# Attention with a conditioning token on one core: six loads of Wk issued by ScalarE, the token's product with Wk placed behind that with Wq, and another split of the first swap round

## The chip, the core and the metric

The kernel runs on one core of one Trainium2 chip. The core has TensorE (PE, with weight loads shown as PEld), VectorE (DVE), ScalarE (ACT), GpSimd (POOL) and SyncE (SP), which only issues transfers. ScalarE and GpSimd can issue transfers too, from their own instruction streams. The metric is the time of one execution in microseconds on the device, as the median of several runs.

## What is computed

The input x has 8 batch elements of 512 rows and 512 columns. There are 16 heads of 32 columns. A conditioning token of 512 numbers per batch element is projected with the same Wq and Wk and added to every row of Q and K:

```python
Q = _split_heads(x @ Wq.T + bq)
K = _split_heads(x @ Wk.T + bk)
V = _split_heads(x @ Wv.T + bv)
tQ = _split_heads(tokens @ Wq.T + bq)
tK = _split_heads(tokens @ Wk.T + bk)
cQ = Q + tQ
cK = K + tK
scores = jnp.einsum('bhqd,bhkd->bhqk', cQ, cK) / jnp.sqrt(jnp.float32(HEAD_DIM))
attn = jax.nn.softmax(scores, axis=-1)
out = jnp.einsum('bhqk,bhkd->bhqd', attn, V)
```

The result, with heads put back beside each other, is added to x. All data are float32.

## The kernel before

**Tasks.** A task t is one batch element and one group of four heads (128 columns), so there are 32 tasks, and t // 4 is the batch element. Each task needs the scores twice: once with queries along the partitions, to get the row maxima (`row_max`, L641 on TensorE, L589 and L650 on VectorE) and the sums of the exponentials (`denominators`, L693 on ScalarE), and once with keys along the partitions, for the product with V (`exponentials`, `weighted`, L808).

**Kept tasks.** For the tasks 2 to 28 (`KEPT`, 27 of them) half of the exponentials are not computed a second time. ScalarE writes them to SBUF in the first pass, VectorE turns them in 32 by 32 blocks (`turn_kept`, L660), and transfers swap the blocks across partitions in place. There are six pairs of places to swap (`APART`), and `swap_kept` does this in three rounds of six copies of 128 KB: round 0 puts one place of a pair aside, round 1 fills it from the other, round 2 fills the other from the copy put aside. Each copy waits for its own pair's copy in the round before. Rounds 0 and 1 of task t + 1 are issued at the end of step t, round 2 in the second third of step t + 1. TensorE reads the kept half in `weighted` of that task, one step later, in the second half of its L808 products. All copies of round 2 are issued by GpSimd; those of round 1 by SyncE; of round 0 SyncE issues the first three pairs and GpSimd the last three (L674).

**The projections.** They use a product scheme with seven block products in place of eight (`first_by_others`, `other_products`, L461). Sums of x blocks for it are made once for each batch element by `combine_x` (L387 to L391) on GpSimd, in the step whose number is 0 modulo 4. GpSimd also scales and adds to the output (L881, L882), adds the bias (L204), splits the maxima (L707 to L710) and makes the sums of a product's parts (L535 to L537, L1220, L1221, L1209). The order of the instructions on each compute engine is the order of the program text. SyncE's transfers are issued in the order that a scheduler gives them.

**The start.** Wq is loaded in four transfers of 128 rows and turned on TensorE (`transpose_w`, L313), with copies to SBUF by ScalarE (L322) and VectorE (L320). The first 128 rows of Wk come through ScalarE's queue and are turned on TensorE too. The other 384 rows come in sixteen loads of 48 KB, in pieces of 128 bytes, so that VectorE alone can turn them (`turn_w`, L963): four quarters cc of the input columns with four row blocks h each (L270). Wv follows in sixteen loads of 64 KB. The token's products are `condition("q")` and `condition("k")` (L902), four small products of which quarter cc needs the turned quarter cc of the weight. Their results are copied by ScalarE (L904), turned back on TensorE (`condition_end`, L889), summed over the quarters and joined with the bias (L911, L917), and then added to Q and K as these leave PSUM (L417, L419). Between them stands the projection of Q for task 1, one quarter at a time (`project_qk_part`, L404). The first row maxima (L641) need K of task 0.

Of the kernel before, what the change touches and what calls it, by code (L numbers as in the profile page):

```python
# [17 lines left out]
def kernel(  # L18
# [38 lines left out]
    nc = tc.nc  # L57
# [5 lines left out]
    HG = P // HD  # L63
    NP = HG // 2
    NS = S // P
    NC = D // P
# [96 lines left out]
    def spread(a, d):  # L163

        return a.rearrange("(f j) d -> j f d", j=BL)[:, :, d : d + BL]

    def load_block(n):

        b, cc = divmod(n, NC)
        if b < B:  # L170
            xs[n] = xp.tile([P, NB, BL], F32, tag="x", name=f"x_{n}")
            for h in range(HG):
                nc.sync.dma_start(xs[n][h * BL : (h + 1) * BL], spread(x[b], cc * P + h * BL))
# [89 lines left out]
    nc.scalar.activation(table, ones[:, :1], AF.Exp)  # L263
    load_w("q", Wq, nc.sync, [2, 3])

    for n, w, f in (("k", Wk, HG), ("v", Wv, 0)):
        wn = ws[n].rearrange("p c (f e) -> p c f e", e=BL)
        for cc in range(NC):
            for h in range(HG):
                nc.sync.dma_start(  # L270
                    wn[h * BL : (h + 1) * BL, cc, f:], spread(w, cc * P + h * BL)[:, f:]
                )
    bvl = const.tile([P, 1], F32, tag="bvl", name="bvl")
    nc.sync.dma_start(bvl, bv.rearrange("(g p o) -> g p o", g=G, o=1)[G - 1])
    bvs = const.tile([P, G, BL], F32, tag="bvs", name="bvs")
# [74 lines left out]
    def transpose_x(n, pt, leaves=nc.vector.tensor_copy):  # L350

        b, sc = divmod(n, NS)
        if b >= B:
            return
        if sc == 0:
            xT[b] = xtp.tile([P, NC, S], F32, tag="xT", name=f"xT_{b}")
        for cc in range(NC):
            nc.tensor.transpose(
                pt[:, cc * P : (cc + 1) * P], xs[n][:, cc * P : (cc + 1) * P], ident
            )  # L360
        leaves(xT[b][:, :, sc * P : (sc + 1) * P], pt.rearrange("p (c s) -> p c s", c=NC))
        if n > 1:
            load_block(n + 2)
# [38 lines left out]
    def project_qk_part(t, n, cc, pt, at=slice(0, S)):  # L402
        b, g = divmod(t, G)
        nc.tensor.matmul(  # L404
            pt[:, at],
            wT[n][:, cc, g * P : (g + 1) * P],
            xT[b][:, cc, at],
            start=(cc == 0),
            stop=(cc == NC - 1),
        )  # L410

    def project_qk_end(t, n, pt):
        b, g = divmod(t, G)
        o = pair_of(t, n)[:, t % 2, :]
        add = tok[:, "qk".index(n), g, b : b + 1]
        if n == "q":
            nc.vector.tensor_scalar(o, pt, add, None, ALU.add)  # L417
        else:
            nc.scalar.activation(o, pt, AF.Identity, bias=add)  # L419
        qkT[n, t] = o  # L420
# [243 lines left out]

    def swap_kept(t, move, last=nc.gpsimd):

        def part(a, g):
            return kept[t][a * BL : (a + 1) * BL, g].rearrange("p c h s -> p (c h s)")

        for n, (a, g) in enumerate(APART):  # L670
            at = (n + 2) % HG * BL
            aside = between[at : at + BL, n // HG].rearrange("p i s -> p (i s)")
            to, of = [(aside, part(a, g)), (part(a, g), part(g, a)), (part(g, a), aside)][move]
            (last if move == 2 or move == 0 and n >= 3 else nc.sync).dma_start(to, of)  # L674

    def denominators(t, qc, w=HG, js=range(HG)):

# [220 lines left out]
    def condition(n, pt):  # L898


        for cc in range(NC):
            nc.tensor.matmul(pt[cc * HD : (cc + 1) * HD, :], condT[:, cc, :], wT[n][:, cc, :])  # L902
        part[n] = early[:, 1 + "qk".index(n), :]
        nc.scalar.copy(part[n], pt)  # L904

    def condition_end(n, pt, on):

        i = "qk".index(n)
        untranspose(part[n], pt)
        sum4 = const.tile([P, NC, B], F32, tag=f"sum4{n}", name=f"sum4_{n}")  # L910
        nc.vector.tensor_reduce(  # L911
            sum4,
            pt.rearrange("p (d c e) -> p d e c", d=NC, c=NC)[:, :, 0:B, :],
            AX.X,
            ALU.add,
        )
        on.tensor_tensor(  # L917
            tok[:, i], sum4, bias2[:, i, :].unsqueeze(2).broadcast_to([P, NC, B]), ALU.add
        )
# [5 lines left out]
    bank = bank_of  # L925
# [4 lines left out]
    def first_part(n, pt, h):  # L930
        for cc in range(NC):
            project_qk_part(0, n, cc, pt, slice(h * HS, (h + 1) * HS))
# [16 lines left out]
    first_part("q", pq, 0)  # L949
    transpose_x(2, bank(0))  # L950
    transpose_x(3, bank(3), nc.scalar.copy)
    first_part("k", pk, 0)
    for half in range(2):
        combine_x(0, half, nc.gpsimd)
# [6 lines left out]
    def turn_w(n, ccs, rows=slice(0, D)):  # L961
        for cc in ccs:
            nc.vector.transpose(wT[n][:, cc, rows], ws[n][:, cc, rows])  # L963

    turn_w("k", range(NC), slice(P, D))
    condition("q", bank(6))
    project_qk_part(1, "q", 0, bank(7))
    condition_end("q", bank(1), nc.vector)
    project_qk_end(0, "q", pq)
    condition("k", bank(5))  # L970
    project_qk_part(1, "q", 1, bank(7))
    condition_end("k", bank(0), nc.gpsimd)
    project_qk_end(0, "k", pk)
# [157 lines left out]
    def thirds(t, made):  # L1131
# [16 lines left out]
        for i in (1, 2):  # L1148
# [6 lines left out]
            if i == 1:  # L1155
                if t + 1 in KEPT:
                    swap_kept(t, 2)
                split_max(t + 1)
                if t + 1 in KEPT:
                    turn_max(t + 1)  # L1160
                else:
                    swap_kept(t, 2)
# [17 lines left out]
            if i == 2:  # L1180
                if r == 0:
                    combine_x(b + 1, 1, nc.gpsimd)
                load_residual(t + 1)
                if t + 1 in KEPT:
                    for move in range(2):
                        swap_kept(t + 1, move)
            else:
                bias_residual(t)
                if r == 0:
                    combine_x(b + 1, 0, nc.gpsimd)  # L1190
# [46 lines left out]
    for t in range(1, T - 3):  # L1237
# [6 lines left out]
        for i, item in enumerate(items):  # L1244
# [3 lines left out]
            w = 0 if alone else HG  # L1248
# [46 lines left out]
    def latest_pair(of, among):  # L1295
        pairs = [(j, j + 1) for j in of if j + 1 in of and among & {j, j + 1}]
        return max(pairs, key=lambda p: order.index(p[0]) + order.index(p[1]))

    last = latest_pair(order, {order[7]})
# [59 lines left out]
    t = T - 3  # L1359
# [20 lines left out]
    t = T - 2  # L1380
# [27 lines left out]
    t = T - 1  # L1408
# [103 lines left out]
```

## Time and profile before

| | us |
|---|---|
| median of 3 runs | 666.72 |
| lowest and highest | 666.71, 668.23 |
| the profiled execution, whole | 667.76 |
| its span in the trace | 666.0 |
| busy: TensorE, VectorE | 652.7 (98%), 589.9 (89%) |
| busy: ScalarE, GpSimd | 542.0 (81%), 423.6 (64%) |

The profile is one execution. Its page gives the busy time of each engine, the chain of work that ended last (followed back from the last instruction, at each step to what released it), the costliest groups of instructions by source line, and the transfers by issuing line. The trace behind it can be asked for timelines, for the chain in a stretch, for waits and for transfers. In a timeline row stand the start in microseconds, the length, the engine, the source line, the operation, what it writes and reads, and in brackets how long the engine was idle before it and what ended that. Matmuls are pipelined and their ends are modelled, so starts are the safer figure on TensorE.

The granted TensorE clock in this execution is 0.996 of full speed over the span.

### The profile page before, as it was taken

How to read it: one execution, taken by the hardware profiler on the slowest of the kernel's cores; microseconds unless marked ns; L12 is line 12 of the kernel's file. 1: busy time of each engine (PE TensorE's matmuls, PEld its weight loads, DVE VectorE, ACT ScalarE, POOL GpSimd, SP SyncE). 2: the span in 40 equal slices, each digit the busy share in tenths (PEclk: the TensorE clock that was granted, in tenths of full speed). 3: DMA queues.
4: the chain of work that ended last, by engine and by line, in shares of the span. 5: the costliest groups of instructions: out<-in, count | busy, mean ns of one | idle time of the engine just before them, and what ended most of it. 6: DMA issues, size and time to landing. Idle time of an engine off the chain costs nothing.

```text
span 666.0 us, 24768 instructions
## 1 busy us (share of the span) xinstructions
PE 652.7 (98%) x9812; PEld 349.4 (52%) x9812; DVE 589.9 (89%) x821; ACT 542.0 (81%) x1378; POOL 423.6 (64%) x668
## 2 busy tenths in 40 slices
PE   9999999999999999999999999999999999999993
PEld 7345445555555555555555555555555555555421
DVE  3698899999999999998999999999999989995793
ACT  2479988889888888988888898888889888887771
POOL 3541345787666876659757696667875597576531
PEclk9999999999999999999999999999999999999998
DMA  6633157778777787877897787779877757786111
GB/s 178 105 51 63 31 122 161 163 165 187 173 152 174 161 190 154 189 156 167 171 190 167 169 191 172 160 150 170 196 165 176 169 133 175 149 181 138 18 18 32
DMA packets 246183, 97.14 MB, mean 146 GB/s; under 512 B 228842, under 2 KB 229354, under 8 KB 246068
## 3 DMA queue, kind: packets, MB, share of 16 engines
q1 hardware_dynamic: 232644, 62.65, 49.3%
q0 software_dynamic: 11664, 31.87, 17.3%
q8 instruction: 77, 1.26, 0.9%
q10 hardware_dynamic: 1760, 1.05, 0.5%
q14 instruction: 38, 0.31, 0.1%
HBM read 19.75 MB, written 8.39 MB: 42 GB/s over the span
## 4 chain that ended last, share of the span: by engine, by line
PE 95%; DMA 2%; SPq 1%; DVE 1%; issue 0%; DVEq 0%
PE psum L461 43%; PE psum L641 19%; PE psum L808 15%; PE psum L777 7%; PE psum L792 3%; PE psum L766 3%; PE psum L748 2%; SPq L270 1%; PE psum L404 1%; DMA w_q<-in_L_cond_Wq_dram 1%; PE psum L745 1%; PE psum L1336 1%; PE psum L818 1%; DMA store<-in_x_dram 1%; DMA w_k<-in_L_cond_Wk_dram 0%; PE psum L843 0%
## 5 line engine op out<-in xcount | busy, mean ns | idle before, releaser
L693 ACT ACTIVATE psum<-psum,nmax 128x512 f32<-128x512 f32 x263 | 174.8, 670 | 5.0 <-DVE nmax L589 3.9
L589 DVE TENSOR_REDUCE nmax<-psum 128x1 f32<-128x512 f32 x219 | 140.5, 678 | 22.2 <-PE psum L641 19.6
L693 ACT ACTIVATE store<-psum,nmax 128x512 f32<-128x512 f32 x190 | 130.3, 700 | 33.3 <-DVE nmax L589 23.8
L650 DVE TENSOR_REDUCE nmax<-psum 128x2 f32<-128x1024 f32 x127 | 153.7, 1211 | 1.3 <-PE psum L641 1.3
L674 POOL DMA_DIRECT2D store<-store x243 | 121.7, 504 | 48.1 <-DMA store<-store 36.2
L641 PE MATMUL psum<-kT,qT 32*128 32x512 f32 x1024 | 146.7, 616 | 0.0
L787 ACT ACTIVATE store<-psum 128x512 f32<-128x512 f32 x216 | 111.5, 603 | 22.6 <-PE psum L777 22.6
L660 DVE STREAM_TRANSPOSE store<-store 128x1024 f32<-128x1024 f32 x108 | 129.5, 1217 | 0.0
L808 PE MATMUL psum<-store,v 128*32 128x256 f32 x1728 | 99.3, 381 | 0.0
L808 PEld LDWEIGHTS psum<-store,v 128*32 128x32 f32 x1728 | 53.2, 110 | 54.1 <-ACT wT_q L628 19.7
L641 PEld LDWEIGHTS psum<-kT,qT 32*128 32x128 f32 x1024 | 57.8, 183 | 37.3 <-issue 20.2
L881 POOL TENSOR_TENSOR res<-res,recs 128x512 f32<-128x512 f32 x30 | 31.4, 1047 | 69.0 <-DVE res L880 68.9
L693 ACT ACTIVATION_READ_ACCUMULATOR psum<-psum,nmax 128x1 f32 x263 | 56.3, 214 | 0.0
L777 PE MATMUL psum<-qT,kT 32*128 32x256 f32 x864 | 55.8, 373 | 0.0
L461 PE MATMUL psum<-wc_v,xc 128*32 128x256 f32 x768 | 47.7, 379 | 0.0
L204 POOL TENSOR_TENSOR xr<-xr,bvs 128x512 f32<-128x512 f32 x30 | 38.4, 1279 | 12.2 <-DMA x<-in_x_dram 11.4
L461 PE MATMUL psum<-xc,wc_k 128*32 128x256 f32 x720 | 44.5, 379 | 0.0
L461 PE MATMUL psum<-xc,wc_q 128*32 128x256 f32 x720 | 44.5, 379 | 0.0
L777 PEld LDWEIGHTS psum<-qT,kT 32*128 32x128 f32 x864 | 42.3, 184 | 3.4
L693 ACT ACTIVATION_READ_ACCUMULATOR store<-psum,nmax 128x1 f32 x190 | 40.8, 215 | 0.0
L882 POOL TENSOR_TENSOR res<-res,xr 128x512 f32<-128x512 f32 x30 | 38.4, 1279 | 2.4
L758 ACT ACTIVATE store<-psum 128x512 f32<-128x512 f32 x56 | 28.9, 603 | 9.3 <-PE psum L748 7.2
(198 smaller groups left out, 1046.3 us busy)
## 6 DMA issues: line engine op xcount, KB each, us to landing
store<-store SPq DMA_DIRECT2D x243, 128.0 KB, 2.8
store<-store POOLq DMA_DIRECT2D x243, 128.0 KB, 3.7
out_dram<-res SPq DMA_DIRECT2D x122, 64.0 KB, 3.6
xr<-in_x_dram SPq DMA_DIRECT2D x120, 64.0 KB, 3.4
x<-in_x_dram SPq DMA_DIRECT2D x112, 64.0 KB, 3.0
w_q<-in_L_cond_Wq_dram SPq DMA_DIRECT2D x4, 256.0 KB, 5.3
w_v<-in_L_cond_Wv_dram SPq DMA_DIRECT2D x16, 64.0 KB, 2.5
w_k<-in_L_cond_Wk_dram SPq DMA_DIRECT2D x16, 48.0 KB, 3.0
```

The source lines that it names most:

```text
L204: nc.gpsimd.tensor_tensor(xr[t], xr[t], bias, ALU.add)
L461: nc.tensor.matmul(pt[r], still[:, r], moving, start=(kc == kcs[0]), stop=(kc == kcs[-1]))
L589: nc.vector.tensor_reduce(nmax[t][:, qc, j : j + 1, 0], pt, AX.X, ALU.max, negate=True)
L641: nc.tensor.matmul(pt, qkT["q", t][r, qc * P : (qc + 1) * P], qkT["k", t][r, :], start=True, stop=True,)
L650: nc.vector.tensor_reduce(nmax[t][:, qc, pr * 2 : pr * 2 + 2, 0], pt, AX.X, ALU.max, negate=True)
L660: nc.vector.transpose(e, e)
L674: (last if move == 2 or move == 0 and n >= 3 else nc.sync).dma_start(to, of)
L693: nc.scalar.activation(to, of, AF.Exp, bias=nmax[t][:, qc, j, :], accum_out=sums[t][:, qc, j, :],)
L777: nc.tensor.matmul(bank[j][:, i * HS : (i + 1) * HS], qkT["k", t][r, kc * P : (kc + 1) * P], qkT["q", t][r, rest], start=False, stop=(i == 1),
L787: nc.scalar.activation(e[:, i, :], bank[pr * 2 + i], AF.Exp)
L808: nc.tensor.matmul(pt[j * HD : (j + 1) * HD, half * HS : (half + 1) * HS], vs[b % 2][:, kc, (g * HG + j) * HD : (g * HG + j + 1) * HD], e, ...
L882: nc.gpsimd.tensor_tensor(y, y, xr.pop(t), ALU.add)
```

## The change

Three things change. First, the loads of Wk and Wv are written as a function, `load_spread`, with a choice of quarters, row blocks and queue. SyncE issues the first ten loads of Wk (quarters 0 and 1 and half of quarter 2) and then Wv. ScalarE issues the other six, and its instruction stream has them behind the copy of the fourth x tile and ahead of its scaled copy of Wq's third part. Second, `condition("k")` moves ahead of the first quarter of the projection and of `condition_end("q")`, so that TensorE has L902 for Wk directly behind L902 for Wq. Third, in round 0 of `swap_kept` GpSimd issues none of the six copies for tasks whose number is 1 modulo 4, and the last five for all others; SyncE has the rest.

```diff
-    for n, w, f in (("k", Wk, HG), ("v", Wv, 0)):
+    def load_spread(n, w, f, ccs, queue=nc.sync, hs=range(HG)):
         wn = ws[n].rearrange("p c (f e) -> p c f e", e=BL)
-        for cc in range(NC):
-            for h in range(HG):
-                nc.sync.dma_start(
+        for cc in ccs:
+            for h in hs:
+                queue.dma_start(
                     wn[h * BL : (h + 1) * BL, cc, f:], spread(w, cc * P + h * BL)[:, f:]
                 )
+
+    load_spread("k", Wk, HG, (0, 1))
+    load_spread("k", Wk, HG, (2,), nc.sync, (0, 1))
+    load_spread("v", Wv, 0, range(NC))
...
     def swap_kept(t, move, last=nc.gpsimd):
 
+        later = 6 if t % 4 == 1 else 1
...
-            (last if move == 2 or move == 0 and n >= 3 else nc.sync).dma_start(to, of)
+            (last if move == 2 or move == 0 and n >= later else nc.sync).dma_start(to, of)
...
     transpose_x(3, bank(3), nc.scalar.copy)
+    load_spread("k", Wk, HG, (2,), nc.scalar, (2, 3))
+    load_spread("k", Wk, HG, (3,), nc.scalar)
     first_part("k", pk, 0)
...
     condition("q", bank(6))
+    condition("k", bank(5))
     project_qk_part(1, "q", 0, bank(7))
     condition_end("q", bank(1), nc.vector)
     project_qk_end(0, "q", pq)
-    condition("k", bank(5))
     project_qk_part(1, "q", 1, bank(7))
```

## The prediction

> **What bounds the kernel now.** I read the chain of waits for the whole span first, then the same chain for single stretches, then the timelines of the engines that it names.
>
> ```profile
> PE 95%; DMA 2%; SPq 1%; DVE 1%; issue 0%; DVEq 0%
> ```
>
> TensorE's own work is 95% of the chain that ends last. An edit elsewhere is therefore worth only what TensorE now waits for. It waits in two kinds of place that the change touches. The first is the start, here in the chain for 0 to 26 us (start, length, what):
>
> ```profile
> 9.87 1.11 SPq L270
> ...
> 11.54 2.07 SPq L270
> ...
> 17.24 2.33 DMA w_k<-in_L_cond_Wk_dram
> ...
> 19.70 0.59 DVE wT_k L963
> ...
> 20.33 1.05 PE psum L902 x2
> 21.38 1.06 PE psum L404 x2
> 22.44 0.44 PE psum L889 x4
> 22.87 1.72 PE psum L404 x4
> 24.59 1.07 PE psum L641 x8
> ```
>
> From 9.87 to 19.57 the end of the chain is SyncE handing out the sixteen loads of Wk one by one, and the flight of the sixteenth. Its turn on VectorE (L963) releases the last quarter of the token's product with Wk (L902) at 20.33. TensorE's timeline of the same stretch shows what ran before:
>
> ```profile
> 16.28 1.06 PE L902 MATMUL psum<-wT_q,condT 128*32 128x512 f32 x8
> 17.28 1.12 PE L404 MATMUL psum<-xT,wT_q 128*128 128x512 f32 x2
> 18.24 0.60 PE L889 MATMUL psum<-ident,store 128*128 128x128 f32 x4
> 18.77 1.06 PE L902 MATMUL psum<-wT_k,condT 128*32 128x512 f32 x6
> ```
>
> Start to start, the product with Wq takes 1.00 us, a quarter of a projection 0.96, the turning back of the token's Q 0.53. From 16.28 to 22.87 there are 6.59 us.
>
> The second place recurs. In one row-maxima burst (L641) per batch element the chain is longer from the fourth time on; the first row is the same burst one batch element earlier, without the excess:
>
> ```profile
> 239.62 0.92 PE psum L641 x8
> ...
> 316.71 1.34 PE psum L641 x7
> ...
> 394.22 1.38 PE psum L641 x6
> ...
> 471.77 1.58 PE psum L641 x8
> ...
> 549.53 1.50 PE psum L641 x8
> ```
>
> The excess over 0.92 is 0.42, 0.46, 0.66 and 0.58, together 2.12 us. The timelines of GpSimd, ScalarE, VectorE and the weight loads around the last one show its cause:
>
> ```profile
> 541.04 1.29 POOL L391 TENSOR_TENSOR xc<-xT,xc 128x512 f32<-128x512 f32 x1
> 541.12 0.66 DVE L880 STREAM_TRANSPOSE res<-psum 128x512 f32<-128x512 f32 x1
> 542.27 1.52 POOL L674 DMA_DIRECT2D store<-store  x3
> 543.32 0.62 ACT L533 COPY qT<-psum 128x512 f32<-128x512 f32 x1
> 543.81 1.06 POOL L881 TENSOR_TENSOR res<-res,recs 128x512 f32<-128x512 f32 x1
> 546.18 0.74 POOL L535 TENSOR_TENSOR qT<-qT 128x256 f32<-128x256 f32 x1
> 547.68 0.73 POOL L537 TENSOR_TENSOR qT<-qT 128x256 f32<-128x256 f32 x1
> 548.45 1.41 DVE L486 SCALAR_TENSOR_TENSOR qT<-psum,tok,qT 128x512 f32<-128x512 f32 x2 [0.26 <-POOL qT L537]
> 549.91 0.29 PEld L641 LDWEIGHTS psum<-kT,qT 32*128 32x128 f32 x2 [0.35 <-DVE qT L486]
> ```
>
> GpSimd works without a pause through the combination of x (L391), three issues of swap copies (L674, 0.51 us each), the scaled output (L881) and the sums of Q (L535 to L537). VectorE waits for the last sum, and TensorE for VectorE to leave the PSUM bank.
>
> **The change, part one: six loads of Wk on ScalarE.** In both kernels' instruction lists a transfer from SyncE or ScalarE waits until the one issued eight places earlier by the two together has landed. The profile shows such a wait at the sixth load of Wk:
>
> ```profile
> SPq L270 <- DMA w_q<-in_L_cond_Wq_dram: 1.0, 1, 1.0
> ```
>
> The new loads stand behind ScalarE's copy of x (L361) and ahead of its scaled copy of Wq (L322):
>
> ```profile
> 9.89 0.58 ACT L361 COPY xT<-psum 128x512 f32<-128x512 f32 x1 [2.99 <-PE psum L358]
> 14.22 0.60 ACT L322 ACTIVATE wT_q<-psum 128x512 f32<-128x512 f32 x1 [3.75 <-PE psum L313]
> ```
>
> They can begin at 10.47 and hide in an idle stretch of 3.75 us. How soon they land is not in the trace; I bound it by the Wk loads issued before and after 13.6 us, in the transfer views of 9.8 to 13.6 and 13.65 to 17.7 us (last column: median from issue to landing):
>
> ```profile
> w_k<-in_L_cond_Wk_dram SPq DMA_DIRECT2D x3, 48.0 KB, 3.6
> ...
> w_k<-in_L_cond_Wk_dram SPq DMA_DIRECT2D x8, 48.0 KB, 2.3
> ```
>
> The first goes out near 10.7 and the second near 11.5, each behind an earlier landing. The fifth waits for the first, the sixth for the second. With 3.6 us of flight the sixth is issued at 15.1 and, with 2.3 of its own, Wk is complete at 17.4. With 2.3 throughout the sixth goes at 13.8; SyncE's tenth load, which waits for its sixth (issued at 9.87, 3.6 in flight: 13.5; up to 14.2 if SyncE's 2.07 us at 11.54 stays), then ends it, at 16.5 at the latest. The other bound is today's 19.57.
>
> What that is worth: a landing L lets TensorE begin the last quarter of L902 at L + 0.76 (19.57 to 20.33 now). Since the product with Wk now stands ahead of the projection quarter and the turning back of Q, 1.05 + 0.96 + 0.53 + 1.06 + 0.44 = 4.04 us follow until the point that is now at 22.87. So the gain is 22.87 - 4.04 - 0.76 - L = 18.07 - L. It cannot exceed TensorE's own work from 16.28: 1.00 + 1.00 + 0.96 + 0.53 + 1.06 + 0.44 = 4.99, so 6.59 - 4.99 = 1.60. L = 17.4 gives 0.7, L = 16.5 gives 1.57, L = 19.57 gives a loss of 1.5: the reordering takes away the 1.49 us of work that now covers the wait. I take 0.8, close to 17.4, since the flights before 13.6 were the long ones.
>
> ScalarE's wait delays L322: issued at 15.1, the sixth load ends near 15.6, so L322 ends at 16.2. TensorE wants it at 16.28. This costs nothing, with only 0.1 us of cover; each later microsecond on ScalarE is one on TensorE. Behind it come only the copies of the token's products. SyncE's loads of Wv and x move up by six issues of about 0.5 us; I find nothing that waits for them now, and if they slow Wk, the bound of 19.57 contains it.
>
> A rule speaks against this part. The Trainium skill, Perfetto Trace Analysis, section "DMA Instruction — HWDGE (DVE, Sync)", says that an issue locks the descriptor generator, which two sequencers share. By it ScalarE's issues would queue behind SyncE's; that is the second rival below. At the start of this trace the two overlap at full speed, which disagrees, though these are loads of 2 KB rows:
>
> ```profile
> 0.73 0.41 ACTq L158 DMA_DIRECT2D store<-in_x_dram  x1
> 0.74 0.41 SPq L231 DMA_DIRECT2D w_q<-in_L_cond_Wq_dram  x1
> ```
>
> **Part two: the first swap round.** For each kept task whose number is 1 modulo 4 (6 of 27), GpSimd loses its three issues of the first round, 1.52 us. That is the stretch shown. L881 can then follow L391 at 542.33, since L880 is done at 541.78; L535 would come at 544.66, after L533 (543.94). Everything to L537 is 1.52 us earlier, more than the excess of at most 0.66, so the four excesses go: 2.1 us. The lower bound is VectorE's own wait, 0.26 in each of four places: 1.0 us. No upper bound above 2.12 is seen. SyncE issues those three copies itself, 1.6 us, and no longer waits for GpSimd's.
>
> In the other 21 tasks GpSimd issues two more, 1.0 us. They hide in the pause in front of L881, as here:
>
> ```profile
> 561.62 1.04 POOL L881 TENSOR_TENSOR res<-res,recs 128x512 f32<-128x512 f32 x1 [2.83 <-DVE res L880]
> ```
>
> Without that cover the cost would be 21 times 1.0. Late next would be the copies themselves; that is the last rival.
>
> **The sum.** The profiled execution took 667.76 us for a span of 666.0, so 1.76 lie around it. Less 0.8 and 2.1 it is 664.9. It is 1.04 above the median of 666.72, so a median run should come at **663.8 us**; the other cases are set against the median too. Its own range, with 0.0 to 1.6 and 1.7 to 2.1, is 663.0 to 665.0.
>
> **Rivals.** (1) Taking GpSimd's lateness away shortens VectorE's wait only, because the bank is then held by the rest of VectorE's queue. For it: the trace names 0.26 us there. Against: the same burst at 239.62 has no excess although VectorE does the same work. Gain 1.0 + 0.8: 664.9, within 0.3%.
>
> (2) The two queues generate descriptors in turn. SyncE's 2.07 us at 11.54 would hold ScalarE's second load until 13.6; alternating at 0.51 us, the sixth would end at 18.2 and land at 20.0. L322 would end at 18.8, and the product with Wk would start its last quarter at 20.76, so the prologue loses 20.76 + 4.04 - 22.87 = 1.9 us. With the 2.1 gained later: 666.5, no change. Against it stand the overlapping issues above.
>
> (3) Slower: the kept exponentials arrive late. A task's third swap round waits for its second and that for its first, and TensorE reads the result half-way through L808. GpSimd's copies land later than SyncE's:
>
> ```profile
> store<-store SPq DMA_DIRECT2D x243, 128.0 KB, 2.8
> store<-store POOLq DMA_DIRECT2D x243, 128.0 KB, 3.7
> ...
> 548.35 2.96 POOL L674 DMA_DIRECT2D store<-store  x6
> ...
> 556.20 3.59 PE psum L808 x64
> ```
>
> Here the third round is issued by 551.31 and lands by 555.0, and is read at 556.20 + 1.8 = 558.0: 3.0 us to spare. Two issues more (1.0) and 0.9 of landing make 1.9, so it does not bite. From 3.0 on each microsecond costs 21: at 3.3 the time is 663.8 + 6.3 = 670.1. For it: the flights differ from burst to burst.
>
> (4) The change does not do what it says at the start: the bound of eight transfers in flight makes ScalarE's loads as late as SyncE's (18.07), so it gains nothing. Then 666.72 - 2.1 = 664.6, just faster.
>
> **How the numbers follow.** Forecast 0.62, rival (1) 0.13, (2) 0.08, (3) 0.12, (4) 0.05. About 0.3%, 2.0 us, is what a measurement can tell from no change, so faster means below 664.7. Of the forecast's cases nine in ten are faster; with most of (4) that makes 0.60. The rest of it, (1) and (2) make 0.28 within 0.3%. Slower is (3). The range runs from 662.4 (both gains whole and 0.6 of scatter) to 667.0, which leaves out (3) and little else.
>
> **What would show it.** Right: a Wk load issued last near 15 us and landing by 17.5; L902 with wT_k directly behind that with wT_q; L641's first burst at 23.0 to 24.0; the four long bursts back at 0.9; GpSimd's L881 straight behind L391 there. Wrong: L322 ending after 16.3, L902 still waiting past 18.8 for L963, the long bursts staying, or L808 split by a wait for copies.

## The result, and the profile after

| | before | after |
|---|---|---|
| median of 11 runs each | 666.71 us | 660.22 us |
| lowest and highest | 665.35, 668.23 | 659.04, 665.05 |
| ratio, 95% interval | | 0.9923, 0.9904 to 0.9942 |
| the profiled execution, whole | 667.76 | 661.76 |
| its span | 666.0 | 659.5 |

The kernel is 6.5 us faster, where 2.9 were forecast, and its time lies below the range. The span was cut at two points, the first burst of row maxima and TensorE's last product. The view of busy time by window gives for each stretch its bounds, its length, and busy time with instruction counts of TensorE, the weight loads, VectorE, ScalarE and GpSimd, then clock, DMA share and GB/s. Before:

```profile
0.00:24.59 24.59, 22.81 (x136) 15.85 (x136) 9.66 (x31) 5.71 (x9) 7.00 (x12) 1.00 0.67 156
24.59:655.56 630.97, 629.93 (x9681) 333.53 (x9680) 579.36 (x788) 536.32 (x1369) 416.64 (x657) 1.00 0.69 147
655.56:666.00 10.44, 0.00 (x1) 0.00 (x0) 0.83 (x3) 0.00 (x0) 0.00 (x0) 0.72 0.24 50
```

After:

```profile
0.00:23.96 23.96, 22.67 (x136) 17.06 (x136) 9.57 (x31) 5.71 (x9) 7.00 (x12) 1.00 0.78 174
23.96:654.90 630.94, 628.12 (x9681) 332.58 (x9680) 579.24 (x788) 536.38 (x1369) 428.63 (x681) 1.00 0.71 146
654.90:659.50 4.60, 0.00 (x0) 0.00 (x0) 0.83 (x3) 0.00 (x0) 0.00 (x0) 0.93 0.55 114
```

The lengths say where the time went. The start lost 0.63 us, the whole steady state 0.03, and the stretch behind TensorE's last product 5.84. That last stretch, in which the engines compute nothing but three short VectorE instructions, is not in the prediction at all. It is called the close below. The granted clock is 1.00 in the first two stretches of both, so it explains nothing here.

**The close.** The view of the line that stands for the program's end lists its instructions (least, median and longest in ns, first and last start). Before:

```profile
L1507 POOLq DRAIN  x3: 34/102/11361, 653.8 to 665.7; - x3
L1507 SPq DRAIN  x3: 7/7/7, 659.3 to 665.5; - x3
L1507 PEldq DRAIN  x2: 13/412/812, 654.8 to 665.5; - x2
```

After:

```profile
L1515 POOLq DRAIN  x3: 34/102/3434, 653.2 to 659.2; - x3
L1515 SPq DRAIN  x3: 7/7/7, 658.6 to 658.9; - x3
```

At the end each engine drains and they meet. GpSimd's longest DRAIN took 11.36 us before and 3.43 after. Its record begins with GpSimd's last sum (653.84; the sum, L1432, runs from 653.88 to 655.15), so 1.3 us of it are that sum. SyncE reaches its own DRAIN, behind the landing of the last stores, 5.45 us after GpSimd's began (653.84 to 659.29; 653.18 to 658.64 after). So a DRAIN of GpSimd's up to about 5.45 us costs nothing here, and before it stuck out by 11.36 - 5.45 = 5.9. SyncE's waits show the same. Before:

```profile
SPq L1507 <- PEq L1507: 6.5, 2, 6.0
```

After:

```profile
SPq L1515 <- PEq L1515: 0.7, 2, 0.5
```

The profile names TensorE's sequencer as the one waited for, but TensorE's DRAIN (the third row of the first listing) was over at 655.6. The engine that was late is the one whose DRAIN is long.

**The start.** The chain of waits for the first 26 us of after:

```profile
7.92 1.93 PE psum L408 x8
...
17.22 2.23 PE psum L908 x16
19.45 1.05 PE psum L408 x2
...
23.96 1.07 PE psum L645 x8
```

Both products of the token run in one piece, no load of Wk is left in the chain, and the first burst (L645, L641 before) comes at 23.96. But TensorE also reached the token's product with Wq later than before, at 17.15 against 16.28. Its first projection product had begun later too, at 7.86 against 6.99; over all profiles of the case that start lies between 6.96 and 8.88, with either order of the loads. The timeline shows the loads of Wk on both queues, ScalarE's copy behind them, and the product:

```profile
8.60 4.03 SPq L270 DMA_DIRECT2D w_k<-in_L_cond_Wk_dram  x6
10.77 5.16 ACTq L270 DMA_DIRECT2D w_k<-in_L_cond_Wk_dram  x6
16.02 0.60 ACT L326 ACTIVATE wT_q<-psum 128x512 f32<-128x512 f32 x1 [4.68 <-DMA w_k<-in_L_cond_Wk_dram]
17.15 1.06 PE L908 MATMUL psum<-wT_q,condT 128*32 128x512 f32 x8
```

**The steady state.** Three of the four long bursts in the chain are back at their short length:

```profile
316.13 0.92 PE psum L645 x8
...
393.23 0.93 PE psum L645 x8
...
549.42 0.92 PE psum L645 x8
```

The fourth, near 471, is not in this chain; in TensorE's timeline it takes 1.02 us (470.17 to the next product at 471.19) where it took 1.69 before (471.60 to 473.29). The four gave 2.1 us, but two new waits took most of them back. TensorE's waits in after:

```profile
PE psum L814 <- DMA store<-store: 1.3, 1, 1.3
PE psum L772 <- DMA maxT<-split: 0.4, 1, 0.4
```

The first is a swap copy that came late. The chain of 505 to 545 us, which begins with what led up to it (L814 was L808):

```profile
503.08 4.48 DMA store<-store
...
510.09 3.99 DMA store<-store
...
515.62 3.06 DMA store<-store
518.68 0.04 issue
518.72 1.93 PE psum L814 x32
```

The first row is SyncE's one first-round copy of this task, and the second is a copy of the second round, which stood behind it in SyncE's queue. The last copy, issued by GpSimd at 515.62, lands at 518.68, and TensorE has waited for it.

### The profile page after: what moved, and what is told of

Its sections match the earlier page's. It is cut to its first block, busy times and chain, and to the rows that moved or that the text cites. A ratio compares the mean times of both kernels' runs of the same rounds, so it can differ in the third digit from the quotient of the medians.

```text
span 659.5 us, 24718 instructions
## 1 busy us (share of the span) xinstructions
PE 650.8 (99%) x9812; PEld 349.6 (53%) x9812; DVE 589.6 (89%) x821; ACT 542.1 (82%) x1378; POOL 435.6 (66%) x692
## 4 chain that ended last, share of the span: by engine, by line
PE 90%; DMA 3%; DVE 2%; SPq 1%; ACT 1%; POOL 1%; issue 1%; DVEq 0%; POOLq 0%
PE psum L465 40%; PE psum L645 17%; PE psum L814 13%; PE psum L783 7%; PE psum L798 3%; PE psum L772 2%; DMA store<-store 2%; PE psum L408 2%; PE psum L754 2%; SPq L680 1%; DMA maxT<-split 1%; ACT store L699 1%; PE psum L751 1%; PE psum L1344 1%; PE psum L824 1%
## 5 line engine op out<-in xcount | busy, mean ns | idle before, releaser
L680 POOL DMA_DIRECT2D store<-store x267 | 133.1, 503 | 44.4 <-DMA store<-store 32.3
L645 PE MATMUL psum<-kT,qT 32*128 32x512 f32 x1024 | 144.4, 615 | 0.0
L814 PE MATMUL psum<-store,v 128*32 128x256 f32 x1728 | 99.6, 381 | 1.3 <-DMA store<-store 1.3
L814 PEld LDWEIGHTS psum<-store,v 128*32 128x32 f32 x1728 | 53.2, 110 | 55.8 <-ACT wT_q L632 19.7
L645 PEld LDWEIGHTS psum<-kT,qT 32*128 32x128 f32 x1024 | 56.6, 183 | 36.3 <-issue 21.6
L887 POOL TENSOR_TENSOR res<-res,recs 128x512 f32<-128x512 f32 x30 | 31.5, 1050 | 49.0 <-DVE res L886 48.9
```

The lines of the kernel that those rows point to most:

```text
L645: nc.tensor.matmul(pt, qkT["q", t][r, qc * P : (qc + 1) * P], qkT["k", t][r, :], start=True, stop=True,)
L680: (last if move == 2 or move == 0 and n >= later else nc.sync).dma_start(to, of)
L814: nc.tensor.matmul(pt[j * HD : (j + 1) * HD, half * HS : (half + 1) * HS], vs[b % 2][:, kc, (g * HG + j) * HD : (g * HG + j + 1) * HD], e, ...
```

## The experiments

Two questions were put: does the DRAIN's length belong to GpSimd's transfers, and what are the two parts worth without it. Runs were compared with runs of the kernel before on the same chip; its median there was 665.0 to 665.9, not 666.7, so ratios are what to compare. Each kernel has one profiled execution. "Theory A" in the expectations says that the change gains by the close alone, and that the DRAIN's length belongs to the number of transfers that GpSimd issued. Unless the text says otherwise each kernel is the kernel after with the line shown.

**One part at a time, and two other splits.** Part one alone:

```diff
-        later = 6 if t % 4 == 1 else 1
+        later = 3
```

> Part one alone: the loads of Wk over both queues and the two products of the token in a row; the swap issues are split as before (GpSimd issues 243 transfers in all, the kernel after issues 267). Theory A (the 5.9 us between the two kernels behind TensorE's last product are GpSimd's final DRAIN, and its length belongs to the set of transfers GpSimd issued: 11.36 us with 243, 3.43 with 267): DRAIN near 11.4 again, TensorE's last product 0.6 us earlier than before (near 654.7), all four long bursts of row maxima stay, median 0.6 below before. Rival B (the DRAIN's length varies from execution to execution whatever the kernel): DRAIN anywhere between 3 and 11, and single times scattered over 660 to 666. Rival C (the close is short because of part one): DRAIN near 3.4 and median 6.5 below before.

Part two alone is the kernel before with the line `later = 6 if t % 4 == 1 else 1` and `n >= later`:

> Part two alone: the kernel before with the new split of the first-round swaps (267 transfers from GpSimd), prologue as before. Theory A: DRAIN near 3.4; the four long bursts gone (2.1 us less), late swap copies and a late DMA transpose in the last third give about 2 us back, so TensorE's last product ends as before (655.4 within 0.5) and the median is 5.9 below before. Rival B: DRAIN anywhere, single times scattered. Rival C: DRAIN near 11.4 and the median within 0.5 of before.

The cut in the six tasks alone, with the new start:

```diff
-        later = 6 if t % 4 == 1 else 1
+        later = 6 if t % 4 == 1 else 3
```

> The kernel after with GpSimd's first-round issues cut in the six tasks t%4==1 as in the change, and the old three in the 21 others (225 transfers from GpSimd). If the four long bursts come from the three issues in those six tasks: they are gone as in the kernel after (2.1 us), and without the extra issues in the 21 others no swap copy is late, so TensorE's last product ends near 652.7 (before 655.4, less 0.6 for part one, less 2.1). Rival: the long bursts go only where the others also issue five, then they stay here and the last product ends near 654.8. The close, by theory A, has one length of its own: with before's 11.36 us DRAIN the median is 664.0, with after's 3.43 it is 658.1.

The other half alone, with the new start:

```diff
-        later = 6 if t % 4 == 1 else 1
+        later = 3 if t % 4 == 1 else 1
```

> The other half of the split: the kernel after with the old three issues of GpSimd in the six tasks t%4==1, and five in the 21 others (285 transfers). Long bursts stay (none of the 2.1 us), and if the late copies come from the extra issues in the 21 others they stay too (2 us): TensorE's last product near 656.8. If the late copies come from SyncE's three more issues in the six tasks, they are gone: near 654.8. The close by theory A again one length of its own; more transfers than after would give 3.4 or less if the length falls with their number, anything else if it depends on their number in another way.

GpSimd's DRAIN, in the same view of the last line, first part one alone (243 transfers):

```profile
L1515 POOLq DRAIN  x3: 34/102/11359, 652.8 to 664.7; - x3
```

Part two alone (267):

```profile
L1509 POOLq DRAIN  x3: 34/102/3434, 651.6 to 658.1; - x3
```

The cut alone (225):

```profile
L1515 POOLq DRAIN  x3: 34/102/9891, 651.9 to 662.3; - x3
```

The other half (285):

```profile
L1515 POOLq DRAIN  x3: 34/102/4906, 652.5 to 658.1; - x3
```

With the same number of transfers the DRAIN is the same to 2 ns, with either start. So it did not vary between these profiled executions, and it does not come from part one. Times and ratios are in the table below. Part one alone is not faster, 1.0009 (0.9995 to 1.0024). Part two alone has 0.9938. e4, which keeps GpSimd's three issues in the six tasks, is as fast as any, 0.9897 (0.9874 to 0.9921). Expectations that failed: e1 kept only two long bursts, e4 one, and e2's last product was 2.2 us earlier than in the profile of before, not the same. The bursts are taken up below.

**More transfers that do nothing.** In the kernel before, one useless swap-sized transfer of GpSimd's per task, in 24 tasks:

```diff
+        if move == 2 and t < 26:
+            of = between[2 * BL : 3 * BL, 0].rearrange("p i s -> p (i s)")
+            nc.gpsimd.dma_start(between[:BL, 1].rearrange("p i s -> p (i s)"), of)
```

> The kernel before with one more transfer of GpSimd's in 24 of its 27 kept tasks, of the size of a swap copy, between two places that nothing reads (267 transfers, as in the kernel after; nothing else changed, no work gained). Theory A (the final DRAIN's length belongs to the number of GpSimd's transfers, 11.36 us with 243, 3.43 with 267): DRAIN 3.4, the span ends 5.9 us earlier than before, less what 24 more issues cost on GpSimd (0 to 1 us): ratio near 0.992, which is the whole change's. Rival (the close got shorter through the other split or its order): DRAIN 11.4 and ratio 1.000. Up to 640 us it is also a second look at the kernel before: long bursts of row maxima near 316, 394, 471 and 549 us again if they belong to its split of the swaps, elsewhere or fewer if they differ from execution to execution.

The same with one element:

```diff
+        if move == 2 and t < 26:
+            nc.gpsimd.dma_start(between[:1, 1, 0, :1], between[2 * BL : 2 * BL + 1, 0, 0, :1])
```

> The same 24 extra transfers of GpSimd's, each of one element of 4 bytes in place of 32 rows of 4096. If the number of transfers counts: DRAIN 3.4 as with the large ones, ratio near 0.992. If their bytes or packets count (a swap copy is 48 packets, 32 of them data): DRAIN between 11.4 and 13.4, ratio 1.000 to 1.003.

The DRAIN was 3.439 us with the large transfers and 3.434 with those of 4 bytes, so bytes do not count and transfers do. The times missed: 1.002 (1.0003 to 1.0037) and 0.9962 (0.9944 to 0.9980). Some bursts of row maxima were longer than any in before. In the chain of e5_pad:

```profile
315.20 1.89 PE psum L641 x8
```

And in that of e7_pad_tiny:

```profile
393.73 1.79 PE psum L641 x8
```

At both VectorE waited for GpSimd's last sum of Q, as the prediction has it. That the 0.5 us of one more issue made them longer is not shown: f1_pad_end below, without an extra issue in the steady state, has a burst of 1.74. Nor do bursts explain the times. The profiled execution of e5_pad, 660.78 us, is the fastest of its twelve, and the others took 664.5 us and more. Where they lost it stands in no trace. It was probably not in the close: all but one have a granted clock of 0.996 to 1.000 over the span, as the kernel after has, and before on the same chip has 0.993 to 0.996. That is only argued.

**Near the fall, and after once more.** The DRAIN grows with the number of transfers and falls once, somewhere between 243 and 267. Four issues in the 21 other tasks:

```diff
-        later = 6 if t % 4 == 1 else 1
+        later = 6 if t % 4 == 1 else 2
```

> The kernel after with four first-round issues of GpSimd in the 21 other tasks in place of five (246 transfers in all). The looks so far give 0.082 us of DRAIN for each transfer (225: 9.89, 243: 11.36; 267: 3.43, 285: 4.91) and one fall of 9.9 us between 243 and 267. If the fall lies below 246: DRAIN between 1.7 and 2.0, ratio 0.988 to 0.992. If above: 11.6, ratio 0.997 to 1.000. Up to TensorE's last product it should have fewer stalls than the kernel after, whose late copies are those of five issues: 627.5 us from 26 us on against after's 629.1.

The kernel after, unchanged:

> The kernel after once more, beside the others on their chip. If its two stalls at 483 us (DMA transpose of the maxima, 0.3) and 518 us (late swap copy, 1.3 to 1.5) belong to its split, they are there again; if they differ between executions, elsewhere or gone. DRAIN 3.43 again. Ratio 0.992 as before.

With 246 transfers the DRAIN is 11.604 us, and a kernel with part one, a split close to part two's and a steady state of 629.1 us, as short as any, is not faster than before at all: 1.0001 (0.9992 to 1.0010). The kernel after has 3.436 and 0.9927 (0.9911 to 0.9942) again. Its two stalls at 483 and 518 us are gone in this execution: they were not fixed to the split.

**Transfers at the end, and fewer transfers.** In the kernel before, in front of L1431; in e6_six_two the same with 24 and with 4:

```diff
     x30 = xr.pop(t - 1)
+    for k in range(24):
+        nc.gpsimd.dma_start(between[:1, 1, 0, k : k + 1], between[2 * BL : 2 * BL + 1, 0, 0, k : k + 1])
```

> The kernel before, with 24 transfers of one element each that GpSimd issues near the end, in the 14.3 us in which it has nothing to do before L1431 (267 transfers in all; no wait and no other work of the steady state is touched). Theory A (the gain of the change is GpSimd's final DRAIN, whose length belongs to the number of its transfers): DRAIN 3.43, the span 5.9 us shorter, 0 to 0.5 us more outside the span, ratio 0.991 to 0.993, as the whole change has. Rival (a part of the change's gain is work done earlier on TensorE): ratio over 0.995.

> The kernel with 246 transfers (GpSimd issues none of the first round in six tasks, four in the 21 others), whose steady state had the fewest stalls, with the same 24 transfers of one element near the end (270 in all). Theory A: DRAIN 3.43 + 3 x 0.082 = 3.7, time 665.2 - 5.4 = 659.8 or a little less, ratio near 0.992 with little spread between executions. Rival (its steady state gains where the close is equal): 0.990 or less.

> The kernel with 246 transfers and four more of one element near the end (250). Where the fall lies: DRAIN near 2.0 if it is at or below 250, 11.9 if above.

All first-round swaps on SyncE:

```diff
-        later = 6 if t % 4 == 1 else 1
+        later = 6
```

> The kernel after with all first-round swaps on SyncE's queue (162 transfers from GpSimd). If the DRAIN goes up by 0.082 us for each transfer and falls by 9.9 us once in about 120 transfers: 162 lies 39 to 42 above the fall, DRAIN 4.7 to 4.8, and the close is short again with fewer transfers than before. If it only falls above some number near 250: 11.36 - 81 x 0.082 = 4.7 as well, so DRAIN cannot tell these two here, but a DRAIN of 3.4 to 3.6 or of 10 and more would speak against both. Time: 5.4 us below before if SyncE's six issues in all tasks cost TensorE nothing, more if copies are late.

The DRAINs came as expected, 3.42, 3.67, 2.05 and 4.74. But f1 and f2 were slower, 1.0055 and 1.0032, and could not answer what they were made for. GpSimd's timeline in f1_pad_end:

```profile
645.90 3.02 POOL L1432 DMA_DIRECT2D store<-store  x6 [8.72 <-DVE acc L1310]
651.40 8.86 POOL L1432 DMA_DIRECT2D store<-store  x18 [2.47 <-issue]
660.26 1.06 POOL L1433 TENSOR_TENSOR res<-res,recs 128x512 f32<-128x512 f32 x1
```

The transfers waited for VectorE until 645.90, and so the last two sums, and with them the stores, came 8 us late. With four (one run) they did fit: 658.73 us. With all swaps on SyncE (f3) the close is short with fewer transfers than before, but TensorE waits for late copies and loads in front of L814, 2.3 us at the longest, and single times scatter from 658.62 to 666.22 (0.9945, 0.9920 to 0.9971).

**The DRAIN alone.** The kernel before, with seven transfers of one element in GpSimd's pause in the start; then with three; then e6_six_two with four:

```diff
     for half in range(2):
         combine_x(0, half, nc.gpsimd)
+    for k in range(7):
+        nc.gpsimd.dma_start(between[:1, 1, 0, k : k + 1], ident[:1, k : k + 1])
```

> The kernel before with seven transfers of one element each from GpSimd in its pause before L917 (about 15.6 to 19.1 of a pause that ends at 23.3 us); 250 transfers in all, nothing else changed. Theory A (all of the change's gain is the close): DRAIN 2.05 as the other kernel with 250, span 5.9 us shorter, 0 to 0.5 us more outside it, ratio 0.991 to 0.993, the same as the whole change's 0.9923 and 0.9927. Rival (part of the gain is in the prologue or in the swaps, as the prediction had it, 2.9 us): ratio near 0.996.

> The control: three such transfers in the same place (246 in all). Theory A: DRAIN 11.60, ratio 1.000 to 1.001. If the extra transfers do something else than moving the DRAIN (wake the queue early, shift the rotation of its eight semaphores), the ratio moves here too.

> The kernel with none of the first-round issues on GpSimd in six tasks and four in the 21 others, and four transfers of one element in the same pause (250 in all). DRAIN 2.05; its steady state had the fewest stalls and its times the least spread (664.5 to 666.2 with the long close), so 659 with a spread under 2 us, ratio 0.990 to 0.992: not slower than the kernel after, and faster if its fewer stalls count.

The last line of g1_pad7, with 250 transfers:

```profile
L1509 POOLq DRAIN  x3: 34/102/2049, 652.7 to 658.7; - x3
L1509 SPq DRAIN  x3: 7/7/7, 658.2 to 658.5; - x3
```

And of g3_pad3, with 246:

```profile
L1509 POOLq DRAIN  x3: 34/102/11602, 653.2 to 665.3; - x3
```

The seven stand in GpSimd's timeline of g1_pad7 here:

```profile
15.67 3.79 POOL L956 DMA_DIRECT2D store<-ident  x7
```

Seven transfers of 4 bytes make the kernel before faster by what the whole change brings: 659.45 us, 0.9908 (0.9892 to 0.9924). Three bring nothing: 1.0012 (0.9996 to 1.0027). The transfers themselves do no work for the output, and from first burst to last product the profile with seven is no shorter than that with three (631.3 and 630.1 us). So the close alone gives a gain as large as the whole change's, and Theory A holds.

All runs together; the fourth column is from the first burst of row maxima to the end of TensorE's last product in the profiled execution:

| kernel | GpSimd's transfers | DRAIN, us | first burst to last product, us | ratio to before |
|---|---|---|---|---|
| f3_all_six | 162 | 4.74 | 636.6 | 0.9945 |
| e3_six_three | 225 | 9.89 | 629.3 | 0.9980 |
| before | 243 | 11.36 | 631.0 | 1 |
| e1_loads_order | 243 | 11.36 | 630.8 | 1.0009 |
| e6_six_two | 246 | 11.60 | 629.1 | 1.0001 |
| g3_pad3 | 246 | 11.60 | 630.1 | 1.0012 |
| f4_six_two_pad4 (one run) | 250 | 2.05 | 629.2 | |
| g1_pad7 | 250 | 2.05 | 631.3 | 0.9908 |
| g2_six_two_pad4 | 250 | 2.05 | 629.1 | 0.9896 |
| after; again | 267 | 3.43; 3.44 | 631.0; 629.1 | 0.9923; 0.9927 |
| e2_swaps | 267 | 3.43 | 629.6 | 0.9938 |
| e5_pad | 267 | 3.44 | 631.4 | 1.0020 |
| e7_pad_tiny | 267 | 3.43 | 632.7 | 0.9962 |
| f1_pad_end | 267 | 3.42 | 631.1 | 1.0055 |
| f2_six_two_pad | 270 | 3.67 | 629.2 | 1.0032 |
| e4_three_one | 285 | 4.91 | 630.7 | 0.9897 |

## Why the prediction was wrong

**The step that failed is the sum.** It took 0.8 and 2.1 from 667.76 us and let everything behind TensorE's last product stand. Of that stretch 5.9 us were GpSimd's DRAIN. Two things were there to be used. The DRAIN of 11.36 us stood in the trace of before. And part two was priced issue by issue, two more of 0.5 us in 21 tasks and three fewer in six, but the balance was never struck: 21 x 2 - 6 x 3 = 24 more transfers, 267 in place of 243. How the DRAIN depends on that number could not be read from one trace. That it would move was not considered, and so no rival and no part of the range held it. Its share of the change in time was put at nothing without a reason, and it measured 5.9. Faster, the likeliest side, came true by luck, for a reason that the prediction did not have.

**Part one: the mechanism came, the gain is not there to be had.** Most signs that the prediction named are in the profile of after: the sixth load on ScalarE (issued at 15.61, landed at 17.58), the products in a row, the first burst at 23.96. The rival of queues that take turns fell: the two queues together issued eight loads from 10.77 to 12.71, one every 0.24 us, where SyncE alone takes 0.51 (13.66 to 17.24 in before). That an issue holds the descriptor generator against the other queue, as the Trainium skill has it (Perfetto Trace Analysis, "DMA Instruction — HWDGE (DVE, Sync)"), does not show in these rows. ScalarE's copy (L322, now L326) ended at 16.62, past the 16.3 that was named as a warning, and cost nothing, because TensorE arrived at 17.15. But the formula 18.07 - L was built on the loads of one execution. From TensorE's first projection product (L404) to the first burst the profile of before has 17.53 us. In the six other executions that have the old start (e2, e5, e7, f1, g1, g3) it is 15.99 to 16.05; there the sixteenth load of Wk is in time, and the chain of e2_swaps is TensorE's own work throughout:

```profile
17.06 1.00 PE psum L904 x8
18.05 1.05 PE psum L404 x2
19.11 0.44 PE psum L891 x4
19.55 0.99 PE psum L904 x8
20.54 1.06 PE psum L404 x2
21.60 0.44 PE psum L891 x4
22.04 1.72 PE psum L404 x4
23.75 1.07 PE psum L641 x8
```

In the ten with the new start it is 15.77 to 16.82, 16.05 in the mean. So the term of 0.8 measured about 0: the interval of e1's timed runs, 0.9995 to 1.0024, leaves room for a gain of 0.3 us at most. The 0.63 us between the two profiles are a stall of one execution.

**Part two: the mechanism was right in the main, the size was that of one execution.** GpSimd's timeline of after has the scaled output (L881, now L887) straight behind the combination of x (L391, now L395), at 542.07 where 542.33 was forecast, and the burst at 549 is short:

```profile
540.84 1.29 POOL L395 TENSOR_TENSOR xc<-xT,xc 128x512 f32<-128x512 f32 x1
542.07 1.06 POOL L887 TENSOR_TENSOR res<-res,recs 128x512 f32<-128x512 f32 x1
```

Each profiled kernel with three GpSimd issues in the six tasks keeps at least one long burst; with none there, all but e2 and f3 have them short. But which of the four are long changes: g3_pad3 has the old split and two of them short,

```profile
317.12 0.92 PE psum L641 x8
...
394.22 0.93 PE psum L641 x8
...
471.33 1.37 PE psum L641 x6
...
548.88 1.50 PE psum L641 x8
```

and its excess is 1.0 us, not 2.1. The profiled executions with the old split and no other stall take 630.1 to 631.3 us from the first burst to the last product, those with six and two 629.1 to 629.2. In timed runs less is left: at equal closes and on the same chip g2 is 0.6 us below g1 (658.82 against 659.45), with intervals that overlap; with long closes, e6 has 1.0001 and g3 1.0012. What the change's own split is worth by itself is not settled: e2, which has it and a short close, stands at 0.9938 (0.9917 to 0.9960), g1, with the old split and a short close, at 0.9908 (0.9892 to 0.9924).

**The slower rival showed itself once.** The prediction gave a copy 3.0 us to spare and took 1.9 of them. In the profile of after one copy was 1.3 us late, by another way than was priced. It belongs to one of the 21 tasks, in which SyncE has only one copy of the first round. SyncE was handing out loads of x (L191) until 502.90 and issued that copy at 503.08, when GpSimd had issued its five by 501.13. It landed at 507.56, the second round waited for it, and GpSimd's third round waited for copies of the second that took 4 us. Why SyncE was that late is open: two tasks earlier it had twelve copies to hand out, but it had them in the second profile of the kernel after too, where TensorE did not wait. It happened in one place, not 21.

## What to carry to other kernels

Read the stretch behind the last compute instruction of the slowest engine as a stage of its own, with a row for each engine's last DRAIN, before any sum is made; where GpSimd issues transfers, count them before and after a change. A stall that stands in one profiled execution is a bound for a gain, not its size: look whether the same burst is short elsewhere in the trace, and take a second profile. Here seven transfers of 4 bytes do for the kernel before what the change does; with the swaps split six and two beside them it was the fastest of those timed together, 658.82 us (0.9896, 0.9878 to 0.9913).

## What the runs showed of the hardware

GpSimd's longest DRAIN, at the end of the program, grows by 0.0817 us with each transfer that GpSimd has issued in the program ((11.60 - 4.74) / (246 - 162); 250 to 285 gives the same) and falls by 9.9 us, 121 such steps, between 246 and 250. It makes no difference whether a transfer moves 4 bytes or 128 KB, nor whether some are issued 15 us after the start (2.049 with 250) or just before the end (2.046 with 250). Up to about 5.45 us (5.1 to 5.8 over the profiles) it is hidden behind the last stores. A trace doesn't show what GpSimd does in that time, and why the length falls is open. Fewer than 162 transfers were not tried; by the same slope the length would come down to the last sum's 1.3 us at about 120, an estimate from these numbers, so below that the line can't hold.

The kernel after also has 2.3 us outside its span where before and g1_pad7 have 1.8, which takes 0.5 of the gain back. e2_swaps, the split alone, has 2.2 as well, and e1_loads_order, the new start alone, 1.8; why was not followed up.

A transfer of one element costs GpSimd the same 0.50 us to issue (18 of them in 8.86 us in f1_pad_end) as one of 128 KB (six in 2.96 us in before).
